# Four residual convolution layers on one core: TensorE products issued in strict pairs, the first layer's mixing as four 64x64 products

## The chip, the cores and the metric

The kernel runs on one core of a Trainium2 chip. The metric is device time in microseconds, the median of several executions. One execution is also profiled; its trace and its page are what this document reads.

## The reference, cut to what matters

The input is x of 16 images, 64 channels, 128 x 128, all in fp32. Four layers follow each other, each of the form x = x + f(group_norm(x)) with 32 groups of two channels:

```python
x = x + conv_w @ (gram(gn(x)) @ gn(x))       # layer 0: gram = xf xf^T / (H*W), 64 x 64 per image
x = x + |sobel_x(gn(x))| + |sobel_y(gn(x))|  # layer 1: Scharr weights 3, 10, 3, per channel
x = x + conv3x3(shift(gn(x)), W) + b         # layer 2: a quarter of the channels shifted left, one right
x = x + clip(leaky(bn(conv1x1(conv3x3(gn(x), w_bin)))), 0, 255)   # layer 3: bn over the whole batch
```

Layer 0 of one image is, once its Gram matrix is known, a product of one 64 x 64 matrix with the image. Layer 3's batch norm needs the sums over all images, so its result can only be applied in a last pass over the data.

## The kernel before, in words

An image lies in SBUF as 128 partitions: the upper 64 rows of every channel on partitions 0 to 63, the lower 64 rows on 64 to 127. A chunk is eight rows of each half, 128 partitions x 1024 elements; an image has eight chunks (`NS`).

The work of all images is one software pipeline, written out by hand. The main loop counts steps, and a step has four quarters q = 0 to 3. In each step one chunk goes through each stage: `Layer3` of image b begins at step 35 + 8b, `Layer2` at 25 + 8b and `Front` (mixing and Sobel, layers 0 and 1) at 15 + 8b. In a quarter the stages are called in the order Layer3, Layer2, Front, then `Gram`, then `tick`, which advances the chains of small operations (the coefficients of the norms). Every engine executes its instructions in exactly this program order. The DMAs of loads and stores are issued on SP's queue, two copies per difference tile on POOL's.

`Gram` of a later image runs ahead. It loads the image with rows on partitions (`load`, tile `xr`), ACT copies each load into `xw` (`rows_to_columns`), and TensorE sums 128 products of 65 columns in three parts (`part`, 44 + 42 + 42) into `pg`. For images 1 to 6 (`EARLY` is 3) a Gram takes four steps (`half`, called with r counting quarters), from image 7 on ten (`at`). `pace` holds the step at which each starts. The stretch until `Front` of image 3 begins is called the fill.

TensorE: nearly every product has 128 rows of contraction and 64 output columns, so it uses one half of the array's columns, and two products, one for each half, can be under way together. `last[0]` remembers the half that was used last; `issue` takes the two lists of products for halves 0 and 1 and alternates, beginning with the half that was not last; when one list is empty, the rest of the other follows. A chunk of layer 2 or 3 is `shared` (three products for each half) and `own` twice (three products for one half, two for the other, since two of its weights are packed into one). Layer 3 has `shared` and the first `own` in q 0, the second in q 1; layer 2 has them in q 2 and q 3. `small_product` is one product for each half.

Mixing (`Front.mix`): x of one chunk is loaded in two DMAs, one per half of the partitions (`Front.load`). In q 1 rows 0 to 3 of the chunk are multiplied with `abd`, a 128 x 128 matrix that holds the same 64 x 64 matrix twice on its diagonal, in q 3 rows 4 to 7. Both use the one PSUM bank of pool `ps_po`. ACT reads it out in `prepare`, in q 2 and in q 0 of the next step, into `xh`. Before an image's first chunk the two rows at the seam of its halves are mixed as `pe`.

[...] `two` 2 x 2, shared by layers 2 and 3, `one`, `po`, one of pool `ps_g` (for `pg` and `pe`) and `bank` for the small products. After the last step the output pass reads layer 3's values and the residual back, applies the batch norm and writes the result.

The engines' calls go through one helper, so the profile shows line 73 for nearly all of them; instructions are told apart by the names of what they write and read (`po<-x,abd` is the mixing, `two<-d,w`, `two<-d,wi` and `two<-qd,pk` are `own`, `one<-v` is `shared`).

Of the kernel before, what the change touches and what calls it, by code (L numbers as in the profile page):

```python
# [10 lines left out]
F32 = mybir.dt.float32  # L11
# [4 lines left out]
B, C, H, W = 16, 64, 128, 128  # L16
P = 128
# [3 lines left out]
R = 8  # L21
NS = HH // R
EARLY = 3
CP = 4
# [84 lines left out]
def tile_kernel(ctx: ExitStack, tc: tile.TileContext, x, cw_h, w2_t, b2, wbin_t, w1_t, b1, gamma, beta, consts, out):  # L109
    nc = tc.nc  # L110
# [5 lines left out]
    small = ctx.enter_context(tc.tile_pool(name="small", bufs=4))  # L116
# [19 lines left out]
    def flat(ap):  # L136
        return ap.rearrange("p j w -> p (j w)")

    def halves(d, h, r0, n):

        v = d[0:C * HW].rearrange("(c r) -> c r", r=HW)
        return v[:, (h * HH + r0) * W:(h * HH + r0 + n) * W]
# [23 lines left out]
    def cols(o):  # L166
        return slice(o * C, (o + 1) * C)
# [3 lines left out]
    def small_product(dst, wt, src):  # L171

        for o in (1 - last[0], last[0]):
            pe.matmul(dst[cols(o)], wt[:, cols(o)], src, start=True, stop=True)
        last[0] = o
# [230 lines left out]
    def gram_product(pg, w):  # L406

        s = w % 2
        pe.matmul(
            pg[s * C:(s + 1) * C, :], xw[:, w // 2, 0:C, s], xw[:, w // 2, :, s],  # L410
            start=(w < 2), stop=(w >= W - 2),
        )
        last[0] = s

    def rows_to_columns(b, m, t):
        act.copy(
            xw[:, :, m * C // 8:(m + 1) * C // 8, :].rearrange("p w c t -> p c w t"),
            t.rearrange("p c (w t) -> p c w t", t=2),
        )
# [38 lines left out]
    class Gram:  # L458
# [21 lines left out]

        def part(self, n):
            if self.w == 0 and n:
                self.pg = ps_g.tile([P, CP, W], F32, tag="g", name=f"pg_{self.b}")[:, 0, 0:C + 1]
            for _ in range(n):
                gram_product(self.pg, self.w)
                self.w += 1

        def load(self, m):
            t = xin.tile([P, C // 8, W], F32, tag="xr", name=f"xr_{self.b}_{m}", bufs=3)
# [2 lines left out]

        def half(self, r):

            if self.b > 1 and 6 <= r < 6 + NS:
                rows_to_columns(self.b, r - 6, self.xr.pop(r - 6))
            if self.b > 1 and 3 <= r < 3 + NS:
                self.load(r - 3)
            self.part({14: 44, 16: 42, 18: 42}.get(r - (self.b == 1), 0))
            if r - (self.b == 1) == 19:  # L500
                chains.append(gram_chain(self.b, self.pg))
# [5 lines left out]
    class Front:  # L507
        first, last = -3, NS

        def __init__(self, b):  # L510
            self.b, self.xs, self.po, self.x2 = b, {}, {}, {}
            self.st = stp.tile([P, 2, NS], F32, tag="st2", name=f"st2_{b}")

        def chunk(self, i):
# [5 lines left out]
        def load(self, i):  # L520
            b = self.b
            t = xin.tile([P, R, W], F32, tag="x", name=f"x_{b}_{i}")
            for h in range(2):
                sp.dma_start(flat(t[h * C:(h + 1) * C]), halves(x[b].rearrange("c h w -> (c h w)"), h, i * R, R))
            self.xs[i] = t

        def mix(self, i, g):
            if self.b == 0 and (i, g) in ((0, 1), (1, 0)):
# [15 lines left out]
        def at(self, i, q):  # L544
            b = self.b
            if q == 0:
                if i == -3:

                    self.xe = xin.tile([P, W], F32, tag="xe", name=f"xe_{b}", bufs=1)
                    sp.dma_start(self.xe[lo], x[b][:, HH, :])  # L550
                    sp.dma_start(self.xe[hi], x[b][:, HH - 1, :])
                    sp.dma_start(x2_d[b][0:W].rearrange("(p w) -> p w", p=1), w0[0:1, 0:W])
                if i + 3 < NS and i + 3 not in self.xs:
                    self.load(i + 3)
                if -1 <= i < NS - 1:
                    self.prepare(i + 1, 1)
                if 1 <= i:
                    self.store(i - 1)
                    act.activation(
                        junk.rearrange("p (j w) -> p j w", w=W), self.x2.pop(i - 1), AF.Square,  # L560
                        accum_out=self.st[:, 1, i - 1:i],
                    )
                if i == NS:
                    chains.append(coefficients(self.st, lambda co: coefs2.update({b: co}), b2_sb))
            if q == 1 and -2 <= i < NS - 2:
                if i == -2:
                    self.abd, self.co = lead.pop(b)
                    self.pe = ps_g.tile([P, CP, W], F32, tag="g", name=f"pe_{b}")[:, 0, :]
                    small_product(self.pe, self.abd, self.xe)
                self.mix(i + 2, 0)  # L570
            if q == 2:
                if i == -2:
                    nc.gpsimd.memset(self.chunk(0)[lo, 0, :], 0.0)
                    self.normalized(self.chunk(0)[hi, 0, 1:1 + W], self.pe[hi], hi)
                    self.pel = small.tile([P, W], F32, tag="pel", name=f"pel_{b}", bufs=1)
                    self.normalized(self.pel[lo], self.pe[lo], lo)
                if i == NS - 2:
                    nc.gpsimd.memset(self.chunk(NS - 1)[hi, R + 1, :], 0.0)
                    act.copy(self.chunk(NS - 1)[lo, R + 1, 1:1 + W], self.pel[lo])
            if 0 <= i < NS:  # L580
                self.sobel(i, q)
            if q == 2 and -2 <= i < NS - 2:
                self.prepare(i + 2, 0)
            if q == 3 and -2 <= i < NS - 2:
                self.mix(i + 2, 1)
                self.xs.pop(i + 2)

# [53 lines left out]
    def taps(o, p, wts, srcs, pad=0):  # L641
# [7 lines left out]
                ))  # L649
        return made  # L650

    def issue(halves):

        n = [0, 0]
        while n[0] < len(halves[0]) or n[1] < len(halves[1]):
            o = 1 - last[0]
            if n[o] == len(halves[o]):
                o = last[0]
            dst, wt, src = halves[o][n[o]]
            n[o] += 1  # L660
            pe.matmul(dst, wt, src, start=(n[o] == 1), stop=(n[o] == len(halves[o])))
            last[0] = o

    def products(p, wts, srcs):
        issue([taps(o, p, wts, srcs) for o in range(2)])
# [269 lines left out]
    for b in range(1, B):  # L935

        pace[b] = at, 2 if b <= 2 * EARLY else 1
        at += NS // pace[b][1] + (2 if b == 2 * EARLY else 0)
    last_one = NS * (B - 1) + starts[0][1]
    steps = last_one + NS + 1  # L940

# [30 lines left out]
    for step in range(starts[2][1] - 2, steps):  # L972
        for q in range(4):
            for b in range(B):

                i = step - starts[2][1] - NS * b
                if 0 <= i < NS and q in (0, 2):
                    live[Front, b].sobel(i, f"first of {q}")
                if q == 3:
                    run(Layer2, b, step - starts[1][1] - NS * b, "first of 3")  # L980
            for stage, at in starts:
                for b in range(B):
                    run(stage, b, step - at - NS * b, q)
            if q == 3:
                for b in range(B):
                    run(Layer2, b, step - starts[1][1] - NS * b, "last of 3")
            for b in range(1, B):
                at, n = pace[b]
                if n == 1:
                    run(Gram, b, step - at, q)  # L990
                elif 0 <= step - at <= 5:
                    live.setdefault((Gram, b), Gram(b)).half(4 * (step - at) + q)

            first = starts[2][1]
            if step == first and q < 3:
                rows_to_columns(1, NS - 3 + q, rows[NS - 3 + q])
            if q == 1 and first + 2 <= step < first + 5:
                weights_of_layer_3(step - first - 2)
            if q == 1 and step == first + 5:
                other_weights()  # L1000
            tick()

            if step == last_one - NS and q == 0:
                slices(xw.rearrange("p w c t -> p (w c t)"), 8)
                slices(xh.rearrange("p a j w -> p (a j w)"), 3)
                rest(xin, "x", [R, W], 2)
                rest(xin, "xr", [C // 8, W], 3)
                rest(work, "u", [R + 1, W + 2], 2)
                rest(work, "e", [R, W + 2], 1)
            if step == last_one and q == 0:  # L1010
                rest(ring, "v2", [(R + 1) * W + 2], 3)
                for t in (diffs["d2"], twins["d2"]):
                    slices(t.rearrange("p n j w -> p (n j w)"), 1)
            if step >= last_one and q == 2:

                n = 3 if step == last_one else 1 if step < last_one + NS - 2 else 0
                rest(ring, "x3", [2, CP, W], NS + 2, n)

            if step >= last_one - NS and q == 3 and len(room) > 1:
                fetch()  # L1020
# [82 lines left out]
```

## Time and profile before

| | before |
|---|---|
| median of 3 runs | 2783.59 us (2782.89 to 2784.94) |
| profiled execution | 2780.96 us, its span 2779.2 us |
| PE busy, share of span, records | 2220.0 us, 80%, 14804 |
| DVE | 2193.7 us, 79% |
| ACT | 2113.9 us, 76% |
| POOL | 837.1 us, 30% |
| mixing, `po<-x,abd` | 1024 records of 512 columns, 351.9 us busy |
| Gram, `pg<-xw` | 4096 records of 65 columns, 148.9 us busy |
| one image in the plateau, with a Gram beside it | 136.4 us |
| one image in the plateau, without | 124.2 us |

Busy times are unions over the whole span; a matmul's end is modelled, so its length says less than the distance between the starts of two that use the same half of the array. An fp32 product stands in the trace as two records. The span has three parts: the fill until about 388 us, the plateau until about 2180, and from about 2330 the output pass.

### The profile page before, as it was taken

The numbers are of one execution on the slowest core, as the hardware profiler recorded it, in microseconds if no ns is written. First come the engines' busy times: TensorE is split into PE (matmuls) and PEld (weight loads), VectorE is DVE, ScalarE is ACT, GpSimd is POOL, SyncE is SP. The second block draws the span as 40 slices with busy tenths as digits, with TensorE's granted clock in tenths as the row PEclk, the third lists the DMA queues.
The fourth block names the chain that finished last, engine by engine and source line by source line (L and its number), as shares of the span: only waits on it lengthen the run. The fifth ranks groups of instructions, "written<-read, shape, count | busy, mean of one in ns | idle before, by whom it ended". The sixth has DMA issues, their size and how long they took to land. (4 is left out here: it accounts for less than half of the span.)

```text
span 2779.2 us, 46241 instructions
## 1 busy us (share of the span) xinstructions
PE 2220.0 (80%) x14804; PEld 1125.6 (41%) x14804; DVE 2193.7 (79%) x3623; ACT 2113.9 (76%) x3177; POOL 837.1 (30%) x1350
## 2 busy tenths in 40 slices
PE   6478899999999999999999999999999995000000
PEld 4234444545454535453535353566666641000000
DVE  5999999898989898989898989999996435333332
ACT  4766889898989898989898988999997667333332
POOL 2054434332333242324242424444444300000000
PEclk8689999999999999999999999999999997555555
DMA  7789888888888888888888867787877768999999
GB/s 200 201 226 233 231 208 232 227 220 221 216 227 223 221 221 222 220 227 215 226 218 223 218 181 204 205 215 208 213 201 188 216 192 285 419 420 420 420 420 390
DMA packets 680289, 685.97 MB, mean 247 GB/s; under 512 B 60096, under 2 KB 580448, under 8 KB 680048
## 3 DMA queue, kind: packets, MB, share of 16 engines
q1 hardware_dynamic: 654896, 613.83, 74.5%
q0 software_dynamic: 25152, 69.18, 10.2%
q8 instruction: 120, 1.97, 0.3%
q14 instruction: 121, 0.99, 0.1%
HBM read 346.23 MB, written 268.44 MB: 221 GB/s over the span
## 5 line engine op out<-in xcount | busy, mean ns | idle before, releaser
L73 PE MATMUL two<-d,w 128*64 128x508 f32 (+2 forms) x2560 | 884.4, 586 | 0.0
L73 PE MATMUL two<-d,wi 128*64 128x508 f32 (+3 forms) x1536 | 616.6, 577 | 0.0
L73 POOL DMA_DIRECT2D qd<-d x512 | 270.8, 531 | 900.5 <-issue 382.2
L73 PE MATMUL two<-qd,pk 128*64 128x512 f32 (+1 forms) x1024 | 518.2, 587 | 5.9 <-DMA qd<-d 5.4
L73 POOL TENSOR_SCALAR edges<-v,co 64x8 f32<-64x8 f32 x512 | 308.4, 602 | 370.4 <-ACT v L73 276.3
L73 PEld LDWEIGHTS two<-d,w 128*64 128x64 f32 x2560 | 299.3, 136 | 279.9 <-issue 202.8
L73 PE MATMUL one<-v,wi 128*64 128x508 f32 (+3 forms) x1536 | 396.6, 596 | 2.5 <-issue 2.5
L73 PE MATMUL one<-v,w 128*64 128x508 f32 (+2 forms) x1600 | 398.1, 578 | 0.5 <-ACT c L73 0.5
L73 PE MATMUL po<-x,abd 128*64 128x512 f32 x1024 | 351.9, 617 | 51.9 <-ACT xh L73 48.9
L73 DVE TENSOR_TENSOR d<-v 128x512 f32<-128x512 f32 (+1 forms) x512 | 346.0, 679 | 38.6 <-ACT qd L73 14.2
L73 ACT COPY qd<-d 64x512 f32<-64x512 f32 x512 | 315.4, 616 | 21.1 <-DVE d L73 14.6
L73 ACT ACTIVATE xh<-po,co 128x128 f32<-128x128 f32 (+1 forms) x480 | 275.1, 621 | 63.7 <-PE po L73 60.5
L73 DVE SCALAR_TENSOR_TENSOR e<-e 128x1032 f32<-128x1032 f32 (+1 forms) x256 | 313.0, 1223 | 0.0
L73 DVE SCALAR_TENSOR_TENSOR y<-two,c 128x1024 f32<-128x1024 f32 x128 | 156.0, 1219 | 133.5 <-ACT v L73 66.4
L73 PEld LDWEIGHTS two<-d,wi 128*64 128x64 f32 x1536 | 193.9, 135 | 153.0 <-issue 109.9
L73 ACT ACTIVATE v<-x,co 128x512 f32<-128x512 f32 (+2 forms) x368 | 234.9, 704 | 0.0
L73 PEld LDWEIGHTS one<-v,w 128*64 128x64 f32 x1600 | 162.3, 137 | 176.3 <-issue 119.7
L73 POOL TENSOR_SCALAR v<-v,kc 128x9 f32<-128x9 f32 x256 | 228.2, 905 | 11.9
L73 PEld LDWEIGHTS one<-v,wi 128*64 128x64 f32 x1536 | 157.2, 139 | 161.6 <-issue 120.0
L73 ACT ACTIVATE u<-u 128x1024 f32<-128x1024 f32 x128 | 135.1, 1055 | 65.3 <-DVE u L73 65.3
L73 DVE SCALAR_TENSOR_TENSOR u<-xh 128x1170 f32<-128x1170 f32 x128 | 175.6, 1372 | 4.7 <-ACT xh L73 3.8
L73 PEld LDWEIGHTS two<-qd,pk 128*64 128x64 f32 x1024 | 130.2, 136 | 111.6 <-issue 72.1
(162 smaller groups left out, 3453.8 us busy)
## 6 DMA issues: line engine op xcount, KB each, us to landing
x<-in_x SPq DMA_DIRECT2D x256, 256.0 KB, 4.0
x_d<-u SPq DMA_DIRECT2D x512, 128.0 KB, 3.7
y_d<-y SPq DMA_DIRECT2D x512, 128.0 KB, 4.1
x_d<-x SPq DMA_DIRECT2D x496, 128.0 KB, 2.5
xr<-in_x SPq DMA_DIRECT2D x120, 512.0 KB, 6.5
qd<-d POOLq DMA_DIRECT2D x256, 130.0 KB, 3.0
qd<-d POOLq DMA_DIRECT2D x256, 129.8 KB, 3.7
v<-x_d SPq DMA_DIRECT2D x448, 72.1 KB, 3.0
```

The costliest lines, as they stand in the source:

```text
L73: return self.tc.keep_in_program_order(call(*args, **kwargs))
```

## The change

- `issue` puts the products into two queues, `held`, and sends them in pairs only, one of each half. What is left of the longer list stays held and is paired with the products of the next call. `issue_rest`, called ahead of `Front` in q 1 and q 3, sends what is still held. `Gram.part` also sends its products in pairs that begin with the half that was not last.
- From image 3 on (`four`) x of a chunk is laid out otherwise: partitions 0 to 63 hold rows 0 to 3 of the chunk and partitions 64 to 127 rows 4 to 7, of both halves of the image. `mix_four` in q 1 multiplies all of it in four products of 64 rows by 64 columns, for two PSUM banks (`ps_po` and `ps_g`); there is no mixing in q 3. `pe` moves from q 1 to q 3 and to pool `ps_po`, its two activations and the POOL memset from q 2 to q 0 of the next step.
- The Gram of images 7 and later is summed in a part of `bank`, and starts one step earlier.
- In `half` the row copies stand at other quarters (r = 3, 4, 5, 7, 8, 9, 11, 12 instead of 6 to 13), and each load is issued three copies ahead, across images too.

```diff
+    held = [deque(), deque()]
+    def emit(o):
+        dst, wt, src, start, stop = held[o].popleft()
+        pe.matmul(dst, wt, src, start=start, stop=stop)
+        last[0] = o
     def issue(halves):
-        n = [0, 0]
-        while n[0] < len(halves[0]) or n[1] < len(halves[1]):
+        for o in range(2):
+            for n, (dst, wt, src) in enumerate(halves[o]):
+                held[o].append((dst, wt, src, n == 0, n + 1 == len(halves[o])))
+        while held[0] and held[1]:
             o = 1 - last[0]
-            if n[o] == len(halves[o]):
-                o = last[0]
-            dst, wt, src = halves[o][n[o]]
-            n[o] += 1
-            pe.matmul(dst, wt, src, start=(n[o] == 1), stop=(n[o] == len(halves[o])))
-            last[0] = o
+            emit(o)
+            emit(1 - o)
+    def issue_rest():
+        while held[0] or held[1]:
+            emit(1 - last[0] if held[1 - last[0]] else last[0])
...
+        def mix_four(self, i):
+            for g, (pool, tag) in enumerate(((ps_po, "po"), (ps_g, "g"))):
+                self.po[i, g] = pool.tile([P, CP, W], F32, tag=tag, name=f"po_{self.b}_{i}_{g}")
+            t = self.xs.pop(i)
+            order = 1 - last[0], last[0]
+            for g in range(2):
+                for h in order:
+                    pe.matmul(self.po[i, g][cols(h)], self.abd[cols(g), cols(g)], t[cols(g), h], start=True, stop=True)
...
         def load(self, i):
+            if self.four:
+                t = t.rearrange("p (h r) w -> p h r w", h=2)
+                v = x[b].rearrange("c (h r) w -> c h (r w)", h=2)
+                for g in range(2):
+                    j = (i * R + g * CP) * W
+                    sp.dma_start(t[cols(g)].rearrange("p h r w -> p h (r w)"), v[:, :, j:j + CP * W])
...
         def part(self, n):
             if self.w == 0 and n:
-                self.pg = ps_g.tile([P, CP, W], F32, tag="g", name=f"pg_{self.b}")[:, 0, 0:C + 1]
-            for _ in range(n):
-                gram_product(self.pg, self.w)
-                self.w += 1
+                if self.b <= 2 * EARLY:
+                    self.pg = ps_g.tile([P, CP, W], F32, tag="g", name=f"pg_{self.b}")[:, 0, 0:C + 1]
+                else:
+                    self.pg = bank[:, 3 * P:3 * P + C + 1]
+            for _ in range(n // 2):
+                for s in (1 - last[0], last[0]):
+                    gram_product(self.pg, self.w + s)
+                self.w += 2
...
         def half(self, r):
-            if self.b > 1 and 6 <= r < 6 + NS:
-                rows_to_columns(self.b, r - 6, self.xr.pop(r - 6))
-            if self.b > 1 and 3 <= r < 3 + NS:
-                self.load(r - 3)
+            if self.b == 2 and r == 0:
+                for m in range(3):
+                    self.load(m)
+            m = {3: 0, 4: 1, 5: 2, 7: 3, 8: 4, 9: 5, 11: 6, 12: 7}.get(r)
+            if self.b > 1 and m is not None:
+                rows_to_columns(self.b, m, self.xr.pop(m))
+                if m + 3 < NS:
+                    self.load(m + 3)
+                elif self.b < 2 * EARLY:
+                    live.setdefault((Gram, self.b + 1), Gram(self.b + 1)).load(m + 3 - NS)
...
-        at += NS // pace[b][1] + (2 if b == 2 * EARLY else 0)
+        at += NS // pace[b][1] + (1 if b == 2 * EARLY else 0)
```

More of the change, by code (lines that the diff above doesn't have):

```diff
@@ L511, in __init__ @@
             self.b, self.xs, self.po, self.x2 = b, {}, {}, {}
+            self.four = b >= EARLY
             self.st = stp.tile([P, 2, NS], F32, tag="st2", name=f"st2_{b}")
@@ L522, in load @@
             t = xin.tile([P, R, W], F32, tag="x", name=f"x_{b}_{i}")
-            for h in range(2):
-                sp.dma_start(flat(t[h * C:(h + 1) * C]), halves(x[b].rearrange("c h w -> (c h w)"), h, i * R, R))
-            self.xs[i] = t
+            if self.four:
[4 more added lines that the diff above has]
+                    sp.dma_start(t[cols(g)].rearrange("p h r w -> p h (r w)"), v[:, :, j:j + CP * W])
+            else:
+                for h in range(2):
+                    sp.dma_start(flat(t[h * C:(h + 1) * C]), halves(x[b].rearrange("c h w -> (c h w)"), h, i * R, R))
+            self.xs[i] = t
+        def mix_four(self, i):
[6 more added lines that the diff above has]
+                    pe.matmul(self.po[i, g][cols(h)], self.abd[cols(g), cols(g)], t[cols(g), h], start=True, stop=True)
         def mix(self, i, g):
@@ L567, in at @@
                     self.abd, self.co = lead.pop(b)
+                if i == -2 and not self.four:
                     self.pe = ps_g.tile([P, CP, W], F32, tag="g", name=f"pe_{b}")[:, 0, :]
                     small_product(self.pe, self.abd, self.xe)
-                self.mix(i + 2, 0)
-            if q == 2:
[L572 to L576, printed above, removed]
+                if self.four:
+                    self.mix_four(i + 2)
+                else:
+                    self.mix(i + 2, 0)
+            if q == 3 and i == -2 and self.four:
+                self.pe = ps_po.tile([P, CP, W], F32, tag="po", name=f"pe_{b}")[:, 0, :]
+                small_product(self.pe, self.abd, self.xe)
+            if (i, q) == ((-1, 0) if self.four else (-2, 2)):
+                nc.gpsimd.memset(self.chunk(0)[lo, 0, :], 0.0)
+                self.normalized(self.chunk(0)[hi, 0, 1:1 + W], self.pe[hi], hi)
+                self.pel = small.tile([P, W], F32, tag="pel", name=f"pel_{b}", bufs=1)
+                self.normalized(self.pel[lo], self.pe[lo], lo)
+            if q == 2:
                 if i == NS - 2:
@@ L583, in at @@
                 self.prepare(i + 2, 0)
-            if q == 3 and -2 <= i < NS - 2:
+            if q == 3 and -2 <= i < NS - 2 and not self.four:
                 self.mix(i + 2, 1)
@@ L981, in tile_kernel @@
             for stage, at in starts:
+                if stage is Front and q in (1, 3):
+                    issue_rest()
                 for b in range(B):
```

## The prediction

> **What bounds the kernel now.** I read the page's busy rows and its 40 slices first, then cut the span at the DVE instruction `e<-xh`, which comes once per chunk, eight times per image, and asked for the busy time of each stretch.
>
> ```profile
> PE   6478899999999999999999999999999995000000
> DVE  5999999898989898989898989999996435333332
> ACT  4766889898989898989898988999997667333332
> DMA  7789888888888888888888867787877768999999
> ```
>
> The last six slices are the output pass, which is all DMA and which the change doesn't touch. Before them lies a long plateau with three engines at eight or nine tenths. The stretches separate them. Columns: window, its length, busy us of PE, PEld, DVE, ACT, POOL, then clock, DMA share, GB/s.
>
> ```profile
> 1335.80:1357.90 22.10, 22.10 (x200) 10.82 (x198) 16.28 (x35) 15.49 (x24) 4.12 (x11) 1.00 0.75 199
> 1357.90:1374.40 16.50, 16.50 (x122) 9.46 (x121) 16.19 (x35) 16.15 (x27) 6.08 (x10) 1.00 0.90 235
> 1426.00:1440.90 14.90, 14.90 (x74) 4.86 (x72) 14.53 (x20) 14.80 (x24) 7.40 (x12) 1.00 0.84 213
> ...
> 1335.80:1472.20 136.40, 135.26 (x927) 62.81 (x925) 126.52 (x219) 122.02 (x191) 46.94 (x83) 1.00 0.84 221
> 1866.10:1990.30 124.20, 124.20 (x632) 79.97 (x630) 120.44 (x180) 113.54 (x181) 57.16 (x83) 1.00 0.81 209
> ```
>
> The fourth row is a whole image with a Gram beside it, the fifth one without. PE is the bound in both, but DVE stands only 10 us (7%) below it in the first and 4 us in the second. The first three rows are steps of the fourth row's image: the step with the Gram's products takes 22.1 us and leaves DVE idle for 5.8, while other steps have DVE and ACT at 97 to 99%. So PE work taken from those steps buys little; in the Gram's step it buys most.
>
> [...] The kernel before never has two row tiles at once, so no run here shows that part. It does show column tiles side by side and mode changes:
>
> ```profile
> 17.12 1.09 PE L73 MATMUL turned<-kc,x_first 128*128 128x128 f32 x8
> 18.14 1.23 PE L73 MATMUL pg<-xw 128*64 128x65 f32 x32
> 19.31 1.09 PE L73 MATMUL turned<-kc,x_first 128*128 128x128 f32 x8
> ```
>
> From 17.12 to 19.31 are 2.19 us. Eight transposes at 0.109 (the spacing inside such a group) take 0.87, and 32 Gram records at 0.031 (84 in 2.64 us later on) take 1.0. The rest, 0.31, is two changes of mode: **0.15 each**.
>
> **The change part by part.**
>
> *Mixing.* An fp32 product stands as two records. A 512-column record holds its half of the array for 0.427 us (1456.95 to 1457.38 below), two halves at a time.
>
> ```profile
> 1456.95 0.59 PE L73 MATMUL two<-qd,pk 128*64 128x512 f32 x1
> 1457.38 0.59 PE L73 MATMUL two<-d,w 128*64 128x512 f32 x1
> ...
> 1457.81 1.44 PE L73 MATMUL two<-d,w 128*64 128x508 f32 x5
> 1458.67 0.34 PE L73 MATMUL pg<-xw 128*64 128x65 f32 x2
> 1459.09 0.59 PE L73 MATMUL two<-d,w 128*64 128x508 f32 x1
> 1459.51 2.95 PE L73 MATMUL pg<-xw 128*64 128x65 f32 x86
> ```
>
> A chunk's mixing is 8 records: 4 x 0.427 = 1.71 us now, 2 x 0.427 = 0.85 if four run at once, plus two mode changes, 0.31. It saves 0.54 a step, 4.4 an image. The bounds: 0.85 if changes cost nothing, -0.31 if row tiles take turns. [...] The second wait for a free `po` bank (q 3) goes too. It cost 1.1 us in the image above and lay in time that ACT or DVE needs anyway: nothing more.
>
> *Pairs.* The rows from 1457.81 show what goes: `own` has three products for one half and two for the other. The third then stands alone when a Gram part follows (1458.67 to 1459.51, the other half idle for 0.84 us). By columns at the rate above, the image's records need 132.1 us of the 135.3 busy; 3.2 are lost, and 0.9 in the image without Gram. So 2.2 an image go (0 to 3.2). The held product runs at the head of the next `own`, a quarter later. DVE's next `d`, which overwrites its operand, is queued behind other DVE work of that quarter, so nobody waits longer.
>
> *Sum for PE:* 135.3 - 4.4 - 2.2 = 128.7 an image with Gram. *DVE* needs 126.5 and keeps 0.15 to 0.37 idle even in its fullest steps (14.90 against 14.53): 127.7 to 129.5. The two now meet. The order on each engine is fixed, so steps don't average out fully. Step by step, with DVE or ACT plus 0.3 in seven steps and 22.1 - 0.5 - 1.7 = 19.9 in the Gram's, the sum is about 133; with free slip it is 128.7. I take the middle, **131, 5.4 less than 136.4**.
>
> *Loads of x.* Each stays two DMAs of 256 KB in sum, now 128 runs of 2 KB instead of 64 of 4 KB. Issues of `y_d<-y`, with 256 runs, take 0.63 us against 0.59 for `x`: 0.04 x 16 an image on SP's queue, which waits for some 13 us of the 136. They land after 4.0 us (page, section 6) and are due over a step later. [...] the stores of `u` in 512 B rows landing in 3.7 us agree. Nothing. The shorter step lifts the DMA share from 0.84 to 0.88, which the window of image 3 already has (0.90).
>
> *Moved steps.* The edge product goes from q 1 to q 3 and its two activations (0.45 each) a half step later, with POOL's memset; they're due before the first Sobel a step on: nothing. If that cover were gone, 0.9 x 13 = 12 us. The Gram's sum in `bank` and its start a step earlier move SP's row loads and the ACT copies by one step, in equal number: 0, give or take 2.
>
> *Fill (to 388 us).* DVE has 24 us idle in 341 here. Six Grams lose pairs, but only the last three beside a busy PE (124.5 of 137.7): 3 x 2, halved for DVE's 124.8, is 3. The row copies (1.18 us each) come where ACT waits for DVE's `u` (44 us in all there), and their loads earlier; of 8.7 us in which ACT waits for `xr`, some 2 reach DVE. Together 5, from -3 to 12.
>
> *The images.* Images 4 to 11: 8 x 5.4 = 43. Image 12 (134.3, DVE 126.3): 4.5. Image 3 (128.5; DVE 123.6, ACT 120.9): 2.5. Images 13 to 15 (355.6; DVE 346.5 and 5 more): 4. Fill 5. Sum 59. The profiled execution took 2780.96 us (span 2779.2 and 1.8 around it), giving 2722; the median of the runs, 2783.6, stands 2.6 above it: **2725**.
>
> **Rivals.**
> *A, as above* (0.63): DVE and PE meet; 2700 to 2752.
> *B, full slip* (0.11): images with Gram come to 128, 8.4 x 8.7 = 73, with the rest 2690. For it: 99% PE beside 97% DVE in the image without Gram. Against: the uneven steps.
> *C, row tiles take turns* (0.13): mixing costs its 1.71 and 0.31 more, 2.5 an image, against 2.2 from pairs. With Gram zero, without Gram +7, fill -5: about 2785, no change. The change then doesn't do what its words say. For it: the trace before has no row tiles.
> *D, slower* (0.11): the mode changes amid dense work cost far more than at 17 us[...]. At s each, a step in an image with Gram gains 0.85 + 0.28 - 2s; it turns at s = 0.56. At 0.8 it loses 0.47 x 70 steps = 33, and without Gram 0.75 x 23 = 17, less 5 in the fill: 2829. For it: from layer 3's small 64x64 products to the next Gram record there are 0.5 us at 95.7. Against: 0.33 of them are marked as a wait for ACT.
> The remaining 0.02 is the unforeseen.
>
> **How the numbers follow.** A measurement of this kernel tells 0.2%, 5.6 us, from no change. A and B are faster, C is split (0.04 faster, 0.06 same, 0.03 slower), D slower: faster 0.79, same 0.07, slower 0.14. The range 2693 to 2788 holds A with its bounds, the near end of B and most of C; D lies outside. Within A alone it is 2700 to 2752.
>
> **What would show it.** Right: `po` records under 64*64, four within 0.2 us and the next four 0.43 later; about 0.15 from the last before to the first of them, and again after; no lone `two` record around `pg`; images with Gram at 129 to 133, PE below 98% and DVE above 96% there. Wrong: `po` groups of 1.7 us (C), gaps of over 0.5 beside them (D), DVE idle growing at `d` for the held product, or SP's queue without waits.

## The result, and the profile after

The changed kernel takes 2778.68 us (median of 20 runs, 2773.79 to 2781.70) beside 2782.88 us for the kernel before in the same set (20 runs, 2779.74 to 2786.01). The ratio is 0.9985 [0.9979, 0.9991]: some 4 us (0.15%) faster, where 59 were forecast. The interval leaves out 1, but the gain is under a tenth of what was expected. The profiled execution took 2778.27 us with a span of 2776.5, 2.7 less than the span before.

The page of the kernel after, its slices:

```profile
PE   6578899999999999999999999999999994000000
DVE  4999999898989898989899999999996435333332
ACT  4766889898989898989898988999997667333332
DMA  8799888988888888888888777878877768999999
```

At this grain nothing has moved. The windows of the trace after, cut at `e<-xh` as before, do show it (image 10, then image 14 without a Gram; columns: window, length, busy us of PE, PEld, DVE, ACT, POOL, then clock, DMA share, GB/s):

```profile
1394.80:1412.40 17.60, 13.45 (x60) 3.78 (x58) 16.95 (x36) 13.74 (x23) 5.48 (x10) 0.94 0.82 226
1412.40:1427.30 14.90, 14.90 (x72) 4.72 (x70) 14.53 (x20) 14.80 (x24) 7.44 (x12) 0.96 0.75 187
...
1442.20:1461.50 19.30, 19.30 (x246) 9.95 (x244) 14.63 (x20) 17.49 (x28) 5.01 (x11) 1.00 0.95 240
1461.50:1479.30 17.80, 17.80 (x165) 7.56 (x162) 14.88 (x21) 13.34 (x20) 5.54 (x11) 1.00 0.72 183
1342.70:1479.30 136.60, 131.64 (x922) 51.73 (x920) 126.42 (x218) 121.84 (x191) 51.12 (x83) 0.99 0.85 223
1867.20:1989.60 122.40, 120.33 (x624) 42.40 (x622) 120.25 (x180) 113.21 (x181) 59.10 (x83) 0.99 0.82 211
```

The image with a Gram is as long as before (136.6 against 136.4). PE needs 3.6 us less in it, DVE exactly what it needed (126.42 against 126.52), and DVE's idle time is unchanged at about 10 us; it only lies elsewhere. The 22.1 us step has gone, and the Gram now fills two steps of 19.3 and 17.8, the rows from 1442.20 and 1461.50, in which DVE idles 4.7 and 2.9. The fourth step has something new, a PE that works only 13.45 of 17.6 us, and a granted clock of 0.94 and then 0.96. The image without a Gram is 1.8 us shorter (124.2 before).

The mixing itself does what the change says. The timeline of PE after (start, duration, line, operation, shape, count):

```profile
1469.62 0.59 PE L73 MATMUL two<-qd,pk 128*64 128x512 f32 x1
1469.62 1.44 PE L73 MATMUL two<-d,w 128*64 128x508 f32 x5
1470.99 1.09 PE L73 MATMUL po<-x,abd 64*64 64x512 f32 x8
1472.01 1.51 PE L73 MATMUL one<-v,wi 128*64 128x512 f32 x6
```

The five records from 1469.62 alternate with their partners and the last starts at 1470.47; by the 0.43 us between two starts on one half, that half is free at 1470.90. The first `po` record follows 0.09 later, four start within 0.02 us, the next four 0.48 after them, and `one` 0.54 after those. From 1470.90 to 1472.01 are 1.11 us; before, two groups of four records took 0.857 each from their first start to that of the next product, 1.71 in all. Of the 101 groups between 400 and 2100 us, the 88 that have `two` ahead and `one` behind start at these distances. No lone `two` record stands around the Gram any more.

### The profile page after: what moved, and what is told of

It reads as the page before. It is cut to its first block, busy times and chain, and to the rows that moved or that the text cites. A ratio compares the mean times of both kernels' runs of the same rounds, so it can differ in the third digit from the quotient of the medians.

```text
span 2776.5 us, 46105 instructions
## 1 busy us (share of the span) xinstructions
PE 2175.3 (78%) x14804; PEld 886.4 (32%) x14804; DVE 2192.0 (79%) x3623; ACT 2112.6 (76%) x3177; POOL 893.2 (32%) x1350
## 5 line engine op out<-in xcount | busy, mean ns | idle before, releaser
L73 PE MATMUL two<-d,w 128*64 128x508 f32 (+2 forms) x2560 | 846.8, 588 | 0.0
L73 PE MATMUL two<-d,wi 128*64 128x508 f32 (+3 forms) x1536 | 578.0, 579 | 0.0
L73 POOL TENSOR_SCALAR edges<-v,co 64x8 f32<-64x8 f32 x512 | 359.9, 703 | 307.7 <-ACT v L73 231.4
L73 PE MATMUL one<-v,w 128*64 128x508 f32 (+2 forms) x1600 | 378.6, 599 | 34.8 <-ACT c L73 34.8
L73 PEld LDWEIGHTS two<-d,w 128*64 128x64 f32 x2560 | 263.1, 136 | 314.9 <-issue 278.5
L73 PE MATMUL one<-v,wi 128*64 128x508 f32 (+3 forms) x1536 | 358.5, 599 | 3.1 <-issue 2.6
L73 ACT COPY qd<-d 64x512 f32<-64x512 f32 x512 | 315.4, 616 | 20.8 <-DVE d L73 14.5
L73 PEld LDWEIGHTS two<-d,wi 128*64 128x64 f32 x1536 | 175.6, 136 | 186.0 <-issue 169.6
L73 ACT ACTIVATE u<-u 128x1024 f32<-128x1024 f32 x128 | 135.3, 1057 | 106.8 <-DVE u L73 106.4
L73 PE MATMUL po<-x,abd 64*64 64x512 f32 (+1 forms) x1024 | 178.5, 643 | 44.0 <-ACT xh L73 41.0
L73 PEld LDWEIGHTS one<-v,w 128*64 128x64 f32 x1600 | 126.0, 139 | 237.9 <-issue 162.7
L73 PEld LDWEIGHTS two<-qd,pk 128*64 128x64 f32 x1024 | 136.3, 136 | 153.9 <-issue 110.6
L73 PEld LDWEIGHTS one<-v,wi 128*64 128x64 f32 x1536 | 108.9, 138 | 224.1 <-issue 209.0
## 6 DMA issues: line engine op xcount, KB each, us to landing
qd<-d POOLq DMA_DIRECT2D x256, 129.8 KB, 3.9
```

Source lines behind the costliest of these rows:

```text
L73: return self.tc.keep_in_program_order(call(*args, **kwargs))
```

## The experiments

All lengths of images and steps come from the DVE marks `e<-xh` in each profiled execution; "the Gram's steps" are the two of an image in which its products stand. Ratios are against the kernel before in the same set; its median lies between 2782.88 and 2783.50 in all sets, so that a difference between sets is good to some 0.6 us. Ahead of each result stands what was expected before the run.

### First set: the held product, the pairs, the place of the Gram

In the image after, DVE waits longest ahead of `d<-v`. The waits of DVE in image 10, before and then after (engine, what waits, what ended it: us, times, longest):

```profile
DVE y L73 <- ACT junk L73: 3.1, 1, 3.1
DVE two L73 <- PE two L73: 2.0, 1, 2.0
DVE y L73 <- ACT u L73: 1.2, 1, 1.2
```

```profile
DVE d L73 <- issue: 5.4, 2, 4.1
DVE y L73 <- ACT e L73: 1.5, 1, 1.5
```

"issue" means that no event in the trace ends the wait, but the timelines after, of PE and of DVE, name the cause:

```profile
1456.03 2.81 PE L73 MATMUL bank<-xw 128*64 128x65 f32 x84
1458.66 1.04 PE L73 MATMUL two<-d,wi 128*64 128x508 f32 x4
```

```profile
1459.77 0.69 DVE L73 TENSOR_TENSOR d<-v 128x512 f32<-128x512 f32 x1 [4.06 <-issue]
```

The products from 1458.66 read the `d` that DVE wants to overwrite. They were held, and 84 Gram records stood ahead of them. So the first theory (H) was that the held product costs what the pairs brought. Its rival (R) was that the order of the steps on the three engines sets the image, and the wait only shows it.

**e1: the held products go out ahead of each Gram part.**

```diff
         def part(self, n):
...
+            if n:
+                issue_rest()
             for _ in range(n // 2):
```

> The changed kernel, but what is held is sent ahead of every Gram part instead of behind it. Theory H (the held product stands behind the Gram's 42 to 44 products, and DVE's next d, which overwrites its operand, waits for it): the 5.3 us per image in which DVE waits before d fall under 1, images 5 to 11 go from 136.6 to 131 to 133.5, the whole to 2731 to 2748 us. Rival R (the order of the steps on DVE, ACT and PE is what limits an image, seen in PE waiting 4.0 us for ACT's c; the wait before d only shows it): DVE's idle time moves to other rows, images stay at 135 to 137, the whole at 2770 to 2785.

Measured: 2790.22 us, 1.0022 [1.0013, 1.0030]. Images 5 to 11 take 136.6, as in the kernel after. DVE's waits in image 10:

```profile
DVE y L73 <- ACT junk L73: 2.8, 1, 2.8
DVE d L73 <- issue: 2.6, 2, 1.3
DVE two L73 <- PE two L73: 1.8, 1, 1.8
```

The 4.1 us wait for the held product is gone, and waits like those of the kernel before stand in its place; the Gram's steps are 15.9 and 21.0. H falls: DVE waits for PE's Gram work, and which product it happens to wait for is secondary. R has the images right, but its 2785 us are exceeded too. The profiled execution was the fastest of its twelve (2778.58); the others lie from 2786 to 2793. The granted clock that each execution records was 0.898 in the profiled one and 0.890 to 0.894 in the others (0.889 to 0.893 in the kernel after), so the others probably had a slow clock once an image, as the kernel after has (second set and last section); no trace of them was kept. Median against median, sending the held product first costs 11.5 us.

**e2: the kernel before with the pairs alone** (`held`, `issue_rest` ahead of `Front`, the Gram's products in pairs).

> The kernel before with the pairs alone (held products, and the Gram's products in pairs): mixing, fill and the Gram's start are those of before. H: DVE waits 4 us or more per image before d here too, and the 2.2 us of PE that pairing saves are lost to it: images with a Gram at 136 to 139, the whole at 2775 to 2805 us. R: no such wait, images at 134, the whole at 2760 to 2770.

Measured: 2782.07 us, 0.9995 [0.9986, 1.0004]. Images 5 to 11: 136.1 to 136.4, against 136.3 before. The Gram's steps are 18.9 and 19.3 instead of 16.3 and 22.1, the same sum within 0.2. DVE waits 4.3 us ahead of `d` here too, and the total lies in H's range; but e1 has taken that wait away and gained nothing. The 2.2 us an image that the prediction took from the pairs do not arrive.

**e3: the kernel after without the pairs** (the old `issue`, the old loop in `part`).

> The changed kernel without the pairs: products of two lists alternate and the rest follows at once, as before; mixing as four, the fill and the Gram's start as changed. H: no wait before d from a held product, images with a Gram at 131.5 to 134, the whole at 2738 to 2760 us. R: images at 135 to 137, the whole at 2770 to 2785. If mixing as four with its two banks were itself what gives the gain back, the same as R.

Measured: 2793.18 us, 1.0038 [1.0025, 1.0051]; images 136.8 to 139.5; the total lies beyond both forecasts. PE still waits 4.0 us for ACT's `c`, so that gap doesn't come from the pairs. With the Gram's early start the pairs are worth 14.5 us.

**e4: the Gram's parts in the odd quarters.**

```diff
-            self.part({0: 44, 2: 42, 4: 42}.get(n, 0))
+            self.part({1: 44, 3: 42, 5: 42}.get(n, 0))
-            if n == 6:
+            if n == 7:
```

> The changed kernel with the Gram parts of images 7 and later one quarter later (q 1, 3, 1 instead of 0, 2, 0), where nothing is held any more; pairs kept, the fill as changed. H: the wait before d goes in images 5 to 11 (not in the fill and image 3), images at 130.5 to 133.5, the whole at 2735 to 2752 us. R: images at 135 to 137, the whole at 2770 to 2785.

Measured: 2808.12 us, 1.0093 [1.0078, 1.0108]; images 139.2 to 140.5; images and total lie beyond both forecasts. The waits of DVE, then PE, in image 10:

```profile
DVE me L73 <- PE bank L73: 4.0, 2, 2.3
DVE d L73 <- issue: 4.0, 1, 4.0
```

```profile
PE bank L73 <- DVE av L73: 3.8, 1, 3.8
```

One quarter's shift of the Gram and of its chain of small operations cost 29 us against the kernel after. DVE now waits for small products in `bank`, and PE for DVE's `av`. This is read from the waits, not tested; it was the hint to look at when the chain runs.

### Second set: the Gram's start, the gap in PE, the Gram itself

This set tests one more theory (T): that the cost lies in the Gram's earlier start. In the fourth step of the image after, two waits of ACT fall together. Its timeline after:

```profile
1399.57 0.49 ACT L73 ACTIVATE v<-x,edge_lower 128x128 f32<-128x128 f32 x1 [1.75 <-DVE edge_lower L73]
...
1404.77 0.20 ACT L73 ACTIVATE sd<-nv 128x1 f32<-128x1 f32 x1 [2.05 <-DVE nv L73]
...
1408.82 0.68 ACT L73 ACTIVATE c<-one,co 128x512 f32<-128x512 f32 x1
```

`sd` is the square root in the Gram's chain. The earlier start puts it into the step in which ACT already waits for `edge_lower`. So ACT comes late to `c`, which frees the one `one` bank, and PE stops. PE's timeline after, the row that waits and the same 12 products three steps on:

```profile
1409.55 4.48 PE L73 MATMUL one<-v,w 128*64 128x512 f32 x12 [4.04 <-ACT c L73]
...
1461.44 2.74 PE L73 MATMUL one<-v,w 128*64 128x512 f32 x12
```

After the stop these products take 4.48 us instead of 2.74: from the third pair on their starts lie 0.85 us apart, not 0.43. That is half speed, and the trace's clock is 0.50 for 3.41 us from 1410.14. Not every stop of PE in these runs is followed by such a stretch; the last section has them.

The other face of it is PE's lead, the time from the start of layer 3's first product to the DVE mark of its step. After, it is 4.9 us ahead of this step, then 3.0, 1.3 and 1.4 when the Gram comes.

**e5: the kernel after, the Gram starting at the step it had before.**

```diff
-        at += NS // pace[b][1] + (1 if b == 2 * EARLY else 0)
+        at += NS // pace[b][1] + (2 if b == 2 * EARLY else 0)
```

> The changed kernel with the Gram of images 7 and later starting at the step it had before (one later than changed). Theory T: the Gram's earlier start puts its chain's square root into the step in which layer 3's edge factors are made; ACT waits twice for DVE there (1.75 and 2.05 us), PE then 4.0 us for ACT's c, and PE comes to the Gram without a lead. Here the two waits stand in different steps: no PE gap of over 2 us, images 5 to 11 at 132.5 to 134.5, the whole at 2748 to 2765 us. Rival S: the 8 us of the Gram's products are added to DVE's time wherever they stand, for PE can't run ahead: images at 135.5 to 137.5, the whole at 2770 to 2785.

Measured: **2767.23 us, 0.9940 [0.9925, 0.9955]**, 11.5 us below the kernel after. Images 134.6 to 135.3; in image 10 the Gram's steps are 18.0 and 18.8, no PE gap is over 2.1 us and the clock doesn't drop (in the whole trace it does so in images 3, 9, 11, 13 and 15, where the kernel after has a drop in each of images 4 to 12); the lead stays at 3.0, 2.9 and 2.6 until the Gram comes. Windows of e5: the first step of image 10, which holds the end of one Gram, its last step, which holds the beginning of the next, and the whole image:

```profile
1332.10:1350.80 18.70, 18.70 (x172) 8.06 (x170) 16.23 (x34) 14.50 (x22) 5.34 (x11) 1.00 0.79 200
...
1448.70:1466.70 18.00, 18.00 (x236) 9.33 (x234) 14.54 (x20) 17.82 (x31) 6.57 (x11) 1.00 0.93 218
1332.10:1466.70 134.60, 130.16 (x922) 51.57 (x920) 126.40 (x218) 122.42 (x192) 51.36 (x83) 1.00 0.87 225
```

T holds in kind; the size was some 2 us beyond its range.

**e6: the kernel after, with twelve unused pairs of small products where the gap is.** They lie in a free part of `bank`, once an image, and only keep PE running.

```diff
+            if q == 0 and step % 8 == 3 and 40 < step < 110:
+                for _ in range(12):
+                    small_product(bank[:, 3 * P:4 * P], k("same"), k("all"))
```

> The changed kernel with twelve pairs of unused 128-column products (2.6 us of PE) in every eighth step, at the place where PE waits 4.0 us for c. After that gap the granted clock is 0.94 to 0.96 and eight records take 2.55 us instead of 1.28. T with the clock as part of it: the clock stays at 1.00, the lead before the Gram grows by 1.3 to 1.7 us and so much comes off the image: 135 us, the whole at 2762 to 2772. S: images at 136 to 137.5, the whole at 2775 to 2785.

Measured: 2769.75 us, 0.9957 [0.9943, 0.9971], 9 us below the kernel after although PE does more. The twelve products of `one` that followed the gap start as late as before, 14.65 us after the mark of their step in both kernels, but take 2.78 us again:

```profile
1399.31 2.81 PE L73 MATMUL bank<-kc 128*64 128x128 f32 x48
1402.15 2.78 PE L73 MATMUL one<-v,w 128*64 128x512 f32 x12
```

The lead stays at 3.0, 2.9, 2.8; the Gram's first step shrinks from 19.3 to 18.0. ACT's two waits are still there. The clock drops in none of images 3 to 11. So most of what the earlier start costs is the slow clock after the gap, not the gap itself: 1.3 us an image, of the 2.0 that e5 gains.

**e7 and e10: four of the Gram's 128 products**, in the kernel after and in the kernel before; the other 124 are left out.

```diff
             for _ in range(n // 2):
-                for s in (1 - last[0], last[0]):
-                    gram_product(self.pg, self.w + s)
+                if self.b <= 2 * EARLY or self.w in (0, W - 2):
+                    for s in (1 - last[0], last[0]):
+                        gram_product(self.pg, self.w + s)
```

> The changed kernel with four of the 128 products of each Gram of images 7 and later (the other 124 are left out; all else is kept). It tells what the 8 us of PE in the Gram's steps cost. S and T: nearly all of them: images at 128 to 130, the whole at 2712 to 2730 us. If instead the chains' waits between DVE and ACT set an image: 133 to 136, the whole at 2750 to 2778.

> The kernel before with four of the 128 products of each Gram of images 7 and later (124 left out, all else kept). If DVE and not PE sets the steps outside the Gram's in the kernel before too, its images come to 129 to 131, close to the changed kernel's 129.5 without these products, and the whole to 2724 to 2742 us: the changed mixing is then worth next to nothing there. If PE sets them, the mixing shows: images at 132 to 134, the whole at 2748 to 2765.

Measured: e7 2721.45 us, 0.9774 [0.9759, 0.9788]; e10 (run with the third set) 2724.76 us, 0.9787 [0.9773, 0.9802]. Image 6 of e7, then of e10:

```profile
782.20:911.70 129.50, 124.41 (x678) 43.90 (x676) 126.26 (x218) 121.16 (x191) 55.13 (x83) 0.99 0.89 232
```

```profile
778.00:907.50 129.50, 128.26 (x675) 56.44 (x673) 126.39 (x219) 121.28 (x192) 50.39 (x83) 1.00 0.90 234
```

DVE's waits in these two images, e7 and then e10:

```profile
DVE d L73 <- POOL v L73: 0.7, 3, 0.2
```

```profile
DVE d L73 <- POOL v L73: 0.7, 3, 0.2
```

This is the pair that settles the case. PE is busy 3.9 us less in the first, although the clock there drops once, yet both images take 129.5. Outside the Gram's products PE isn't what sets the time, though it is busy 99% of it in e10: DVE waits for PE, for ACT or for a DMA in neither, and its 126.3 with some 3.2 of short gaps make the image. (All of images 5 to 11 take 129.5 to 129.6 in e7, 129.5 to 130.6 in e10.) The other six steps show it too: in image 10 they take 16.5, 18.5, 16.7, 16.4, 14.9 and 14.9 us in the kernel before as in e10. So the Gram's 8 us of PE work costs 6.8 us of an image before (136.3 - 129.5), 7.1 after, and 5.1 in e5, and this cost is all that any saving on PE could ever have brought in these images.

**e8: the Gram in six parts of 20 and 22 products instead of three.**

> The changed kernel with the Gram of images 7 and later in six parts of 20 to 22 products over six quarters, instead of three of 42 to 44 over five. If the length of one part is what DVE's d runs into (2.6 us behind the held product): the wait before d falls from 4.1 to under 2 us and images to 132 to 134.5, the whole at 2745 to 2765 us. S: the same 8 us in the same step and a half, images at 135.5 to 138, the whole at 2770 to 2790.

Measured: 2779.35 us, 0.9985 [0.9978, 0.9992], images 136.6: the kernel after again. How long one part keeps PE from DVE's products made no difference here.

### Third set: the best version, and each part alone

**e9: e5, and e1's line for the Grams of the fill only** (`if n and self.b <= 2 * EARLY`).

> The changed kernel with the Gram's start as before and, for the Grams of the fill (images 1 to 6), what is held sent ahead of each part. In the fill PE isn't full, so the held product only delays DVE's d there (9.0 us of waits to 392 us): if so the fill ends 2 to 4 us earlier than with the later start alone (391.4) and the whole comes to 2763 to 2766 us. If the fill is set by other waits: 390.5 to 392 and 2766 to 2769.

Measured: 2763.28 us, 0.9925 [0.9909, 0.9942], the fastest of the kernels that do all the work. The total is in the first range, but the fill doesn't end 2 to 4 us earlier as forecast: 391.2 against 391.4 in e5, with its first mark 1.2 later (47.8 against 46.6). Images 2 and 3 are shorter, 136.4 and 129.8 against 138.0 and 131.1.

**e11: everything but the pairs, with the Gram's old start** (e3 and e5 together).

> Mixing as four, the changed fill and the Gram's sum in bank, with the Gram's start as before and without the pairs. Of PE's savings only those in the Gram's step and a half count: two steps of mixing there, about 1 us, and no pairs: images at 135 to 137, the whole at 2770 to 2785 us. If mixing as four is worth its full 4 us of PE: images at 132 to 134, the whole at 2745 to 2760.

Measured: 2779.08 us, 0.9984 [0.9977, 0.9991], images 136.3.

**e12: the kernel before with the new row copies and loads of the fill alone.**

> The kernel before with the fill's row copies and loads alone. Image 0 took 1.6 us more with them in the changed kernel, images 1 and 2 were held up by other things. If the copies by themselves help: the fill ends at 384 to 387 instead of 388.2 and the whole is 2779 to 2782 us. If they cost: 389 to 391 and 2784 to 2787.

Measured: 2781.69 us, 0.9996 [0.9988, 1.0005]. The fill ends at 390.4, 2.2 later than before, but its first mark already stands 2.7 later; image 2 within it is 2.4 shorter. There is no measurable effect on the whole.

With the Gram's old start, the two main parts stand against each other so:

| | median, us | image with Gram | the Gram's two steps |
|---|---|---|---|
| neither (before) | 2783.2 | 136.3 | 16.3 + 22.1 = 38.4 |
| pairs (e2) | 2782.1 | 136.2 | 18.9 + 19.3 = 38.2 |
| four at once, bank and fill (e11) | 2779.1 | 136.3 | 16.2 + 22.2 = 38.4 |
| both (e5) | 2767.2 | 134.6 | 18.0 + 18.8 = 36.8 |
| Gram of four products, before (e10) | 2724.8 | 129.5 | 14.9 + 16.6 = 31.5 |

The lengths are medians of images 5 to 11; e10's is that of image 6 (median 129.7). Each part alone gives these images 0.1 us or nothing; both together give 1.7 us. What the four products do is visible in the lead: with them PE reaches the Gram 2.6 to 2.7 us ahead (e5, e11), without them 1.4 (before, e2). Why e11 doesn't turn that lead into time was not separated; its lone third products still stand behind the Gram, and DVE waits 2.0 us for a `two` there, as before.

## Why the prediction was wrong

Predicted and measured against the profiled spans, by stretch (us):

| stretch | predicted | after | e5 |
|---|---|---|---|
| fill | -5 | +3.9 | +3.2 |
| image 3 | -2.5 | +3.8 | +2.6 |
| images 4 to 11 | -43 | -0.3 | -12.3 |
| image 12 | -4.5 | -5.4 | -3.4 |
| images 13 and 14 (predicted: 13 to 15) | -4 | -2.8 | -2.8 |
| the rest | 0 | -2.0 | -1.1 |
| sum | -59 | -2.7 | -13.7 |

- **Mixing: right.** Four at once, 1.11 us with both mode changes against a forecast 1.16, 0.60 saved a step against 0.54. Rivals C and D are excluded by the same rows, although C's total came true. The two `po` changes took 0.09 and about 0.11 us (0.54 less the 0.43 of a record) instead of 0.15. That a group takes 0.85 was my estimate, since the trace before has no row tiles at once; in the trace after, four records start within 0.02 us, all eight within 0.50.
- **The images without a Gram: right in size.** Images 13 to 15 went from 355.6 to 352.1, 3.5 of the forecast 4. But "PE is the bound" was too much here too. In image 14 before, PE was busy for 124.2 of 124.2, and still DVE had only two waits over 0.25 us, 0.93 at 1973.0 and 0.71 at 1988.4. The trace names POOL's `v`, which had ended 0.5 us or more earlier, so the waits were probably for the PE products that read `d`; the next products on their half start at 1973.01 and 1988.41. These two waits are gone after, and the image takes 122.3, DVE's 120.25 and 2.1 of short gaps. Mixing alone does it (e11: 122.3); with the pairs alone it stays at 124.2 (e2).
- **The sum for PE in an image with Gram: 1.5 us low.** Forecast 128.7; e5, which has the change without the slow clock, is busy for 130.16.
- **The failed step: "I take the middle, 131", between free slip (128.7) and step by step (133).** Neither was a bound: e5 takes 134.6, more than both. (Added up from its own rows, step by step is 133.8, not 133.) DVE with its short gaps sets 129.5, the upper end of the prediction's own range for it, even when the Gram is all but gone (e7, e10), so 131 required a Gram of 1.5 us where it costs 6.8. I read "PE is the bound" off 135.26 of 136.40 and so charged every step's saving to the image. But the steps without the Gram were DVE's, and a faster PE there only waits. Its lead can't be saved up for the Gram either: in e5 it is 5.5 us at the fourth step and 2.6 when the Gram comes, since PE has waited 4.4 us in between for ACT's `c` and DVE's `av`. The sentence "PE work taken from those steps buys little; in the Gram's step it buys most" was right, and the sum then didn't keep to it. Of the 5.6 us between 131 and 136.6, e5 puts 2.0 on the Gram's start. The other 3.6 are the 1.5 above and PE idle time, 4.4 us in e5 where the middle had left 2.3.
- **The second failed step: "its start a step earlier ... 0, give or take 2".** It cost 11.5 us (e5). I had counted instructions that move, and not what each of them waits for: the square root waits for DVE, and behind it on ACT is the read that frees PE's bank.
- **"So nobody waits longer" for the held product: wrong as stated, small in effect.** DVE waits 4.06 us for exactly that product. Taking the wait away (e1) only moved it, so this was not the cause.
- **The fill: nothing gained.** +3.9 stands in the table instead of -5, but its sign isn't clear of the variation: e10 is the kernel before up to there and ended its fill at 391.8 (388.2 in the trace before), and the kernel after, e6, e7 and e8, alike up to there, at 390.9 to 392.9. The copies and loads alone gave nothing (e12). In the trace after, DVE has four waits of 9.0 us in sum ahead of `d` in the fill, where the trace before has 0.5 of that kind; sending the held product first (e9) gives back 1.6 in image 2 and 1.3 in image 3.
- **Image 12: right by accident.** In the kernel before, the last Gram's final 98 records fall into image 12; after, they all fall into image 11. The work was moved, not saved. Image 3 pays for it: 159 records of the first such Gram before, all 256 after. The pairs alone do the same in small, +3.1 in image 3 and -2.8 in image 12 (e2).
- **Slips in the working that change little.** The two loads of a chunk are 256 KB each, not in sum. B's 73 and the other 16 us give 2695, not 2690.

What stays open: why e4's shift by a quarter costs 29 us, and why the mixing's lead brings nothing without the pairs (e11).

## What to carry to other kernels

An engine that is busy 99% of a stretch needn't be its bound when a neighbour with a fixed order stands at 97% in the same steps; leave the suspected work out in both versions first, and see how short the stretch gets (here 129.5 us in both), because that floor is all that can be gained. Price a saving in the step in which the other engine really waits, and nowhere else. When a start moves by a step, go through the waits of every instruction that moves, on every engine: here two waits of 1.75 and 2.05 us that fall together on ACT stopped PE for 4.04 us, and the slow clock after it cost more than the stop (9 us by e6, of the 11.5 by e5).

## What the runs showed of the hardware

After the idle time of 4.04 us the next products ran at half rate for some 3 us (starts 0.85 us apart instead of 0.43). In e1 a stop of 3.4 us at the same place left the rate as it was, while in e7 two stops of 1.8 and 2.4 us, with 1.9 us of products between, were followed by starts 0.78 and 0.84 us apart (ten products in 3.60 us). So in these runs the length of one gap doesn't decide it.

The clock of the traces shows more. In all fourteen it changes only on a grid of 3.41 us; before and after have 21 and 43 changes, each within 0.001 us of a multiple of 3.413 from the first. Stretches of that grid around the stop in image 10, after, then e1, then e7 (columns: window, length, PE busy, clock, DMA share, GB/s):

```profile
1406.73:1410.14 3.41, 0.59 (x4) 1.00 0.81 217
1410.14:1413.55 3.41, 3.41 (x12) 0.50 0.65 151
```

```profile
1408.00:1411.41 3.41, 1.46 (x8) 1.00 0.82 219
1411.41:1414.83 3.42, 3.42 (x20) 1.00 0.56 124
```

```profile
1364.78:1368.20 3.42, 1.03 (x8) 1.00 0.59 168
1368.20:1371.61 3.41, 3.41 (x12) 0.50 0.89 220
```

With PE busy for 17% and 30% of a stretch the next one is slow; with 43% in e1 it isn't. Over all traces, from 390 to 2300 us, 64 stretches at full clock were followed by half clock, and PE was busy for at most 43% of each; 7686 were not, and it was busy for at least 41% of each. (Before and after hold 10 of the first, with at most 42%, and 1097 of the others, with at least 48%.) So in these traces the border lies at 41 to 43% of PE time in a stretch, and for the gaps measured here it matters where the grid cuts them. An image of 136.6 us is 40 such stretches (136.5), so the grid cuts the gap at nearly the same place in image after image: the kernel after is slowed in all of images 4 to 12, from image 5 on every 136.5 us (at 727.5, 864.0 and so on to 1683.2), the profiled execution of e1 in none of images 5 to 12.

Filling the gap with twelve useless pairs of products (e6) made the kernel 9 us faster.

In the trace before, the instructions of DVE, ACT and POOL start in the order of the kernel's calls: 2950, 1975 and 470 groups of like ones, none out of place. On PE the records of neighbouring products, one of each half, alternate.
